# Counting a state space product as 6.0 units instead of 2.2 when attention tiles are handed out beside it

## The chip, the core and the metric

The kernel runs on one core of a Trainium2 chip, in one launch. The metric is the device time of that launch in microseconds (us); smaller is better. Engines are named as the profile names them: PE (TensorE, matmuls and transposes), DVE (VectorE), ACT (ScalarE), POOL (GpSimd) and SP (SyncE, which here only issues DMAs). L757 is line 757 of the kernel before.

## The reference, cut to what matters

Two layers of a small model on `x` of shape (2, 1024, 256), float32. Each of the four blocks reads a layer norm of `x` and is added to `x`:

```
x = x + attention(ln(x))      # 16 heads of 128, causal, linear bias by key position
x = x + ternary_ffn(ln(x))    # gated, hidden width 1024, weights quantized per group of 64
x = x + state_space(ln(x))    # in_proj 256->1024, conv of 4 taps, 512 channels x 16 states
x = x + kept_two_ffn(ln(x))   # gated, 1024 wide, of every 4 hidden values the 2 largest are kept
```

The state space block runs, for every channel d and state n, the recurrence

```
h[t] = exp(delta[t] * A[d, n]) * h[t-1] + delta[t] * B[t, n] * u[t, d]
y[t, d] = sum over n of h[t] * C[t, n]
```

Attention of a query needs all earlier keys of its sequence; the three other blocks need only the rows themselves and, for the state space, the state carried from the rows before.

## The kernel before

**Chunks and stages.** The 2 x 1024 rows are cut into four chunks of 512 rows: chunks 0 and 1 are the first and second half of sequence 0, chunks 2 and 3 those of sequence 1. Attention (`attention`, a generator) runs over the chunks in order, inside a chunk over 16 heads, inside a head over 4 tiles of 128 queries: 64 tiles to a chunk. One tile is scores on PE (L362), a clip with the mask on DVE (L366), the bias added and the row's extreme taken on DVE (L372, one instruction with two operands in SBUF), the exponential on ACT (L377), and two tiles later the transposes on PE (L293). Once a head there come the values (L304), the output projection (L318), its addition to `x` on DVE (L324), and the projections to q, k and v of the next head (L335, L342). Chunks 1 and 3 look back over 512 to 1024 keys and are called heavy here; chunks 0 and 2 look back over up to 512 keys and are called light.

While attention works on chunk k, the three other blocks of chunk k-1 (`rest`, also a generator) are interleaved with it. So there are five stretches: stage 0 (attention of chunk 0 beside the quantization of weights), stages 1, 2 and 3 (attention of chunks 1, 2 and 3 beside `rest` of chunks 0, 1 and 2), and a last stretch with `rest` of chunk 3 alone. In stage 1 and stage 3 the attention is heavy, in stage 2 it is light.

**What `rest` holds.** `ternary_ffn`: weights from DRAM through POOL's queue (L459), layer norm, 8 gated pieces (L441, `g_f` and `u_f`), and 64 matmuls back to width 256 (L502, `fo`). `state_space`: layer norm, `in_proj` (L608), the convolution as 4 DVE instructions for each of 4 channel groups (L624, L626), `dtl` and `bcp` (L639, L648), then `steps` for each channel group (a chain over PE, ACT, DVE and POOL, L544 to L575), then the 64 products (4 channel groups x 16 states), then the output projection (L816, `mo`). `kept_two_ffn`: layer norm, 8 gated pieces (L441, `g_g` and `u_g`), 6 comparisons (L924) and 12 further instructions on DVE (`keep_two`, L880 to L882), then the projection (L932, `go`) and the store of the result.

**A product** passes all engines: a row of B and a row of C are loaded, each spread over 128 partitions (SP's queue), `enter` multiplies on POOL (L736, `db`), `decay` makes the factors on ACT (L750, `da`), `scan` runs the recurrence on DVE (L757, `hs`), `keep` copies the last column on DVE (L766) where the sequence goes on, `weigh` multiplies by C on POOL (L771, `hc`), and `total` adds up on PE with 4 transposing matmuls (L701, `y`). These steps are staggered: `total` of a product is emitted 5 or 6 products after its `decay` (`DRAIN`).

**What sets the order.** Both generators say how far they are. The driver at L970 to L978 takes one tile of attention at a time, and after tile i of 64 runs `rest` until its emitted units reach the share (i + 1)/64 of the whole:

```
            whole = cost(k - 1)
            while done < whole * (i + 1) / (H * UT):
                done += next(r, whole)
```

Every `yield` in `rest` gives its units: 3 for a gated piece of the first ffn, 4 for one of the last, 2 for a quarter of an output projection, 2.2 for each product. `cost` (L952) adds up the same units for a whole `rest`. This order of emission is not yet the order on the engines: a scheduler builds each engine's instruction list from it, taking first what was emitted first among what it holds to be ready, and `tc.issue_after` adds constraints (a scan is held behind the L372 of the tile before the last one). Each engine then works through its own list in order. Weights of a block are loaded when the space of the block before is free.

Of the kernel before, what the change touches and what calls it, by code (L numbers as in the profile page):

```python
# [20 lines left out]
KC = D // P  # L21
NT = S // P
LAG = 2
FF = 1024
NFC = FF // P
GRP = 64
DI, DN, DR, DC = 512, 16, 128, 4
NDC = DI // P
NX = DR + 2 * DN
U = 512  # L30
UT = U // P
# [10 lines left out]
def kernel(  # L42
# [108 lines left out]

    guT_d = dr.tile([P, KC, 2 * FF], F32, tag="guT_d", name="guT_d")
    prT_d = dr.tile([P, NFC, D], F32, tag="prT_d", name="prT_d")

    def quantize(pool, key, src):
# [19 lines left out]
        yield  # L175
        q = pool.tile([P, n], BF16, tag="q", name=f"q_{key}", bufs=2 * FF // (2 * P) + FF // D)
        m = pool.tile([P, n], BF16, tag="m", name=f"m_{key}")
# [8 lines left out]
    def quantized_weights(pool):  # L186
        def put(key, q, dst):
# [12 lines left out]
            (f"gu{r}", w_gu[r : r + 2 * P, :].rearrange("(a p) d -> p a d", p=P), guT_d[:, :, r : r + 2 * P])  # L200
            for r in range(0, 2 * FF, 2 * P)
        ] + [
# [3 lines left out]
            )  # L206
            for c in range(0, FF, D)
        ]
# [77 lines left out]
    def turn(k, h, j, s, st):  # L286

        qi = CH[k][1] * UT + j
        for kb0 in range(0, qi + 1, 4):
            n = min(4, qi + 1 - kb0)  # L290
            tp = ps_mm(f"pt_{k}_{h}_{j}_{kb0}").rearrange("p (c t) -> p c t", c=4)
            for i in range(n):
                nc.tensor.transpose(  # L293
                    tp[:, i, :], s[:, (kb0 + i) * P : (kb0 + i + 1) * P], ident
                )
            nc.any.tensor_copy(st["pts"][kb0 // 4][:, 0:n, j * P : (j + 1) * P], tp[:, 0:n, :])  # L296

    def values(k, h, st):
        u = CH[k][1]
        zp = ps_z(f"z_{k}_{h}")  # L300
        last = (u + 1) * UT - 1
        for kb in range(last + 1):
            q0 = max(0, kb - u * UT) * P
            nc.tensor.matmul(  # L304
                zp[:, q0:], lhsT=st["v_all"][:, kb, :],
                rhs=st["pts"][kb // 4][:, kb % 4, q0:], start=(kb == 0), stop=(kb == last),
            )
        st["z"] = a2.tile([P, U], F32, tag="z", name=f"zs_{k}_{h}")
        nc.any.tensor_copy(st["z"], zp)  # L309

    def project(k, h, st):

        rr = a3.tile([P, UT], F32, tag="rr", name=f"rr_{k}_{h}")
        nc.vector.reciprocal(rr, st["rs"])
        for t in range(0, UT, 2):
            op = ps_mm(f"o_{k}_{h}_{t}").rearrange("p (a m) -> p a m", a=2)
            for i in range(2):
                ended["by"] = nc.tensor.matmul(  # L318
                    op[:, i, :], lhsT=st["z"][:, (t + i) * P : (t + i + 1) * P], rhs=st["o"],
                    start=True, stop=True,  # L320
                )
            for i in range(2):
                xt = x[k][:, t + i, :]
                nc.vector.scalar_tensor_tensor(  # L324
                    xt, op[:, i, :], rr[:, t + i : t + i + 1], xt, op0=ALU.mult, op1=ALU.add
                )
# [28 lines left out]
    def scores(k, h, j, st):  # L355

        W = (CH[k][1] * UT + j + 1) * P
        s = a3.tile([P, S], F32, tag="s", name=f"ss_{k}_{h}_{j}", bufs=4)
        for k0 in range(0, W, 512):
            n = min(512, W - k0)  # L360
            sp = ps_s(f"s_{k}_{h}_{j}_{k0}")
            nc.tensor.matmul(  # L362
                sp[:, :n], lhsT=st["qT"][:, j * P : (j + 1) * P], rhs=st["kT"][:, k0 : k0 + n],
                start=True, stop=True,
            )
            nc.vector.scalar_tensor_tensor(  # L366
                s[:, k0 : k0 + n], sp[:, :n], CLIP, lower[:, S - W + k0 : S - W + k0 + n],
                op0=ALU.min, op1=ALU.max,
            )
        nm = a3.tile([P, 1], F32, tag="nm", name=f"nm_{k}_{h}_{j}")  # L370
        pace["front"] = tiles[-2] if len(tiles) >= 2 else None
        pace["tile"] = nc.vector.tensor_tensor_reduce(  # L372
            out=s[:, :W], in0=s[:, :W], in1=st["alibi"][:, :W], scale=1.0,
            scalar=3.0e38, op0=ALU.add, op1=ALU.min, accum_out=nm,
        )
        tiles.append(pace["tile"])
        nc.scalar.activation(  # L377
            s[:, :W], s[:, :W], AF.Exp, bias=nm, scale=-1.0, accum_out=st["rs"][:, j : j + 1]
        )
        return s  # L380

    def attention():
# [7 lines left out]
        for i, (k, h) in enumerate(heads):  # L390
# [8 lines left out]
            for j in range(UT):  # L399
                s = scores(k, h, j, st)  # L400
                later.append((LAG, lambda a=(k, h, j, s, st): turn(*a)))
                if j == UT - 1:
                    later.append((LAG, lambda a=(k, h, st): values(*a)))
                    later.append((LAG + 1, lambda a=(k, h, st): project(*a)))
                if j == UT - 1 and h == H - 1:
# [45 lines left out]
    def ternary_ffn(k):  # L451
        with ExitStack() as fctx:
# [3 lines left out]
            f2 = fctx.enter_context(tc.tile_pool(name="f2", bufs=2, side="right"))  # L456
            guT = fw.tile([P, KC, 2 * FF], F32R, name=f"guT_{k}")
            prT = fw.tile([P, NFC, D], F32R, name=f"prT_{k}")
# [56 lines left out]
    DRAIN = lambda k: 5 if k + 1 < len(CH) and CH[k + 1][1] == 0 else 6  # L515

    def state_space(k):
# [5 lines left out]
        with ExitStack() as mctx:  # L523
# [20 lines left out]
            def steps(c):  # L544

                vp = ps_r(f"dt_{k}_{c}")
                ended["by"] = nc.tensor.matmul(
                    vp, lhsT=dt_sb[:, c * P : (c + 1) * P], rhs=dtl, start=True, stop=True
                )


                v = row_of("sv", f"sv_{k}_{c}", 1)
                e = row_of("se", f"se_{k}_{c}", 1)
                with tc.issue_after(marks[0].ins):
                    nc.scalar.activation(e, vp, AF.Abs, bias=dt_bias(c))
                relu = lambda: nc.scalar.activation(v, vp, AF.Relu, bias=dt_bias(c))

                idle = tail_end and c == 0
                if not idle:
                    relu()  # L560
                nc.scalar.activation(e, e, AF.Exp, scale=-1.0)
                l = row_of("dl", f"dl_{k}_{c}", 2)
                log = nc.scalar.activation(l, e, AF.Ln, bias=one)
                if idle:
                    with tc.issue_after(log.ins):
                        relu()
                r = work(f"sr_{k}_{c}")
                nc.vector.tensor_scalar(r, e, 1.0, -1.0, ALU.add, ALU.add)  # L568
                marks.append(nc.vector.tensor_tensor(r, e, r, ALU.subtract))
                (nc.vector if idle else nc.gpsimd).tensor_tensor(l, l, r, ALU.add)  # L570
                dl = l
                (nc.vector if short or idle else nc.gpsimd).tensor_tensor(dl, v, l, ALU.add)
                du = row_of("du", f"du_{k}_{c}", 2)
                marks.append((nc.vector if idle else nc.gpsimd).tensor_tensor(du, dl, xs[:, c, :], ALU.mult))
                return dl, du  # L575

            def turned(c, du):

                tp = ps_r(f"dup_{k}_{c}")
                for t in range(UT):  # L580
                    nc.tensor.transpose(
                        tp[:, t * P : (t + 1) * P], du[:, t * P : (t + 1) * P], ident
                    )
                duT = row_of("duT", f"duT_{k}_{c}", 2)
                nc.scalar.copy(duT, tp)
                return duT
# [213 lines left out]
            for i in range(-5, len(prods) + DRAIN(k)):  # L800
                for lag, f in stages:
                    if 0 <= i - lag < len(prods):
                        f(i - lag)
                if i >= 0:
                    yield 2.2
                if 0 <= i < len(prods) and i // DN + 1 < NDC:
                    c = i // DN + 1
                    if i % DN == (DN // 4 if tail_end else DN // 2):
                        parts[c] = steps(c)
                        yield 3  # L810
                    if tail_end and i % DN == DN - 5:
                        turns[c] = turned(c, parts[c][1])
# [134 lines left out]
    def rest(k):  # L947
        yield from ternary_ffn(k)
        yield from state_space(k)
        yield from kept_two_ffn(k)  # L950

    def cost(k):  # L952

        own = 3 + 3 * NFC + 2 * UT + 3 + 5 * NDC + 4 + 3 * NDC + 2.2 * (DN * NDC + DRAIN(k)) + 2 * UT
        return own + 3 + 4 * NFC + 1.3 * 6 + 2.5 * 4 + 4 * UT


# [90 lines left out]
```

## Time and profile before

| | us |
|---|---|
| median of 3 runs | 1836.12 |
| lowest and highest run | 1835.04, 1838.70 |
| span of the profiled execution, first to last instruction | 1836.9 |
| PE busy | 1718.3 (94% of the span) |
| DVE busy | 1218.3 (66%) |
| ACT busy | 963.7 (52%) |
| POOL busy | 832.2 (45%) |

The page gives no time of the profiled execution beside its span; the span lies between the lowest and the highest run, so nothing of note lies around it. A share of busy time is a mean over stretches with different limits, so the stretches have to be read one by one. Two cautions go with PE: its instructions are pipelined and overlap in the records, so the mean duration of a matmul is more than the distance from its start to the next one's, and gaps shorter than that overlap are counted as busy. In the answers below "mean ns" is the recorded duration of one instruction, and "x" the number of records; a float32 matmul makes two records.

### The profile page before, as it was taken

What the parts mean: (1) busy time and instruction counts of PE and PEld (TensorE: products, weight loads), DVE (VectorE), ACT (ScalarE), POOL (GpSimd) and SP (SyncE); (2) the same over time, 40 slices, a digit from 0 to 9 for tenths busy, and PEclk for the clock granted to TensorE, in tenths of its full rate; (3) what the DMA queues carried; (4) which work ended last, traced back from release to release, by engine and by line L of the source; (5) the groups of instructions that cost most, each with busy time, mean ns of one, the idle gap of its engine ahead of it and who ended that gap; (6) DMA issues with size and microseconds to landing.
All of it is one profiled execution on the core that took longest, in us unless ns stands there. A gap on an engine that the chain in (4) does not pass through costs nothing. (4 is left out here: it accounts for less than half of the span.)

```text
span 1836.9 us, 24217 instructions
## 1 busy us (share of the span) xinstructions
PE 1718.3 (94%) x7956; PEld 1144.2 (62%) x7956; DVE 1218.3 (66%) x2349; ACT 963.7 (52%) x1789; POOL 832.2 (45%) x674
## 2 busy tenths in 40 slices
PE   7999999998999999998888999999999999998899
PEld 4666666555656557755555667756656565566895
DVE  5666555777785473458886565557788655667975
ACT  3444474656563553555554545566555446446742
POOL 3324032588892000419998000418898500035870
PEclk9999999999999999999999999999999999999999
DMA  6443512466662311337787324227665430212541
GB/s 201 128 142 128 193 46 88 149 203 204 216 202 91 103 52 48 125 109 232 245 247 224 116 71 141 82 67 228 226 214 184 142 115 26 75 53 86 178 136 57
DMA packets 178301, 255.99 MB, mean 139 GB/s; under 512 B 16240, under 2 KB 90992, under 8 KB 177152
## 3 DMA queue, kind: packets, MB, share of 16 engines
q1 hardware_dynamic: 176752, 241.61, 41.4%
q0 software_dynamic: 1152, 12.58, 1.9%
q8 instruction: 63, 1.03, 0.2%
q14 instruction: 62, 0.51, 0.1%
q10 hardware_dynamic: 272, 0.26, 0.0%
HBM read 232.04 MB, written 22.35 MB: 138 GB/s over the span
## 5 line engine op out<-in xcount | busy, mean ns | idle before, releaser
L771 POOL TENSOR_TENSOR hc<-hs,cs 128x512 f32<-128x512 f32 x256 | 362.1, 1428 | 10.8 <-DVE ss L366 3.1
L362 PE MATMUL s<-kT,qT 128*128 128x512 f32 (+3 forms) x768 | 302.7, 495 | 19.9 <-DVE ss L366 18.0
L377 ACT ACTIVATE ss<-ss,nm 128x128 f32<-128x128 f32 (+7 forms) x256 | 198.8, 776 | 183.5 <-DVE nm L372 174.1
L366 DVE SCALAR_TENSOR_TENSOR ss<-s,lower 128x512 f32<-128x512 f32 (+3 forms) x384 | 204.6, 549 | 121.0 <-PE s L362 119.4
L736 POOL TENSOR_TENSOR db<-du,bs 128x512 f32<-128x512 f32 x192 | 259.2, 1356 | 44.4 <-DVE hs L757 30.6
L304 PE MATMUL z<-pT,v 128*128 128x512 f32 (+3 forms) x768 | 264.5, 492 | 10.9 <-ACT pT L296 10.2
L372 DVE CUSTOM_DVE_ANT_0 ss<-ss,alibi 128x128 f32<-128x128 f32 (+7 forms) x256 | 241.3, 945 | 3.5
L750 ACT ACTIVATE da<-dl,a_neg 128x512 f32<-128x512 f32 x256 | 177.9, 698 | 115.6 <-DVE hs L757 90.6
L304 PEld LDWEIGHTS z<-pT,v 128*128 128x128 f32 x768 | 142.8, 190 | 145.1 <-issue 92.7
L296 ACT COPY pT<-pt 128x512 f32<-128x512 f32 (+3 forms) x321 | 145.4, 474 | 162.0 <-PE pt L293 160.4
L293 PE MATMUL pt<-ident,ss 128*128 128x128 f32 x1152 | 180.3, 279 | 32.1 <-DVE x L324 18.5
L293 PEld LDWEIGHTS pt<-ident,ss 128*128 128x128 f32 x1152 | 140.0, 142 | 94.7 <-DVE x L324 33.0
L362 PEld LDWEIGHTS s<-kT,qT 128*128 128x128 f32 x768 | 127.9, 193 | 84.1 <-issue 43.4
L757 DVE TENSOR_TENSOR_SCAN hs<-da,db 128x512 f32<-128x512 f32 x128 | 153.8, 1210 | 38.6 <-ACT da L750 20.8
L757 DVE TENSOR_TENSOR_SCAN hs<-da,carry,db 128x512 f32<-128x512 f32 x128 | 159.1, 1269 | 24.4 <-POOL hc L771 14.7
L324 DVE SCALAR_TENSOR_TENSOR x<-o,rr,x 128x256 f32<-128x256 f32 x256 | 108.9, 476 | 76.7 <-PE o L318 76.5
L701 PE MATMUL y<-ident,hc 128*128 128x128 f32 x1024 | 144.8, 279 | 8.4 <-POOL hc L771 8.4
L342 PEld LDWEIGHTS pv<-wv,xT_a 128*128 128x128 f32 x1024 | 124.4, 192 | 37.1 <-issue 25.3
L342 PE MATMUL pv<-wv,xT_a 128*128 128x128 f32 x1024 | 125.8, 275 | 5.5 <-ACT zs L309 3.4
L701 PEld LDWEIGHTS y<-ident,hc 128*128 128x128 f32 x1024 | 121.0, 145 | 14.3 <-POOL hc L771 11.9
L318 PE MATMUL o<-wo,zs 128*128 128x256 f32 x512 | 125.4, 386 | 4.1 <-ACT kT L338 3.0
L335 PE MATMUL pq<-xT_a,wq 128*128 128x512 f32 x256 | 122.7, 601 | 0.7 <-ACT xT_a L148 0.7
(204 smaller groups left out, 2468.7 us busy)
## 6 DMA issues: line engine op xcount, KB each, us to landing
cs<-bcd SPq DMA_DIRECT2D x256, 256.0 KB, 3.8
bs<-bcd SPq DMA_DIRECT2D x192, 256.0 KB, 4.3
alibi<-alibi_d SPq DMA_DIRECT2D x32, 512.0 KB, 4.2
wq<-in_wqT_dram SPq DMA_DIRECT2D x64, 128.0 KB, 3.5
wk<-in_wkT_dram SPq DMA_DIRECT2D x64, 128.0 KB, 3.1
wv<-in_wvT_dram SPq DMA_DIRECT2D x64, 128.0 KB, 2.8
wo<-in_woT_dram SPq DMA_DIRECT2D x64, 128.0 KB, 2.8
alibi<-alibi_d SPq DMA_DIRECT2D x32, 256.0 KB, 3.6
```

Source lines behind the costliest of these rows:

```text
L293: nc.tensor.transpose(tp[:, i, :], s[:, (kb0 + i) * P : (kb0 + i + 1) * P], ident)
L304: nc.tensor.matmul(zp[:, q0:], lhsT=st["v_all"][:, kb, :], rhs=st["pts"][kb // 4][:, kb % 4, q0:], start=(kb == 0), stop=(kb == last),)
L342: nc.tensor.matmul(vp[:, t, :], lhsT=xT[:, c, t * P : (t + 1) * P], rhs=st["v"][:, c, :], start=(c == 0), stop=(c == KC - 1),)
L362: nc.tensor.matmul(sp[:, :n], lhsT=st["qT"][:, j * P : (j + 1) * P], rhs=st["kT"][:, k0 : k0 + n], start=True, stop=True,)
L366: nc.vector.scalar_tensor_tensor(s[:, k0 : k0 + n], sp[:, :n], CLIP, lower[:, S - W + k0 : S - W + k0 + n], op0=ALU.min, op1=ALU.max,)
L372: pace["tile"] = nc.vector.tensor_tensor_reduce(out=s[:, :W], in0=s[:, :W], in1=st["alibi"][:, :W], scale=1.0, scalar=3.0e38, op0=ALU.add, ...
L377: nc.scalar.activation(s[:, :W], s[:, :W], AF.Exp, bias=nm, scale=-1.0, accum_out=st["rs"][:, j : j + 1])
L701: nc.tensor.matmul(yTs[c][:, t * P : (t + 1) * P], lhsT=h[:, t * P : (t + 1) * P], rhs=ident, is_transpose=True, start=start and t == 0, s ...
L736: nc.gpsimd.tensor_tensor(db[i], du, brow.pop(i), ALU.mult)
L750: nc.scalar.activation(da[i], parts[c][0], AF.Exp, scale=a_neg[:, c, n : n + 1])
L757: nc.vector.tensor_tensor_scan(out=hs[i], data0=da.pop(i), data1=db.pop(i), initial=0.0 if first else carry[:, n, c : c + 1], op0=ALU.mult ...
L771: nc.gpsimd.tensor_tensor(hc[i], hs.pop(i), crow.pop(i), ALU.mult)
```

## The change

A named constant takes the place of the literal 2.2, in both places that have to agree: in what `state_space` yields after each product, and in what `cost` adds up for it. Its value is 6.0. No instruction is added, removed or altered by it; it decides after which attention tile each piece of `rest` is emitted. By the driver's arithmetic a whole `rest` goes from about 305 units to about 571, a tile's share from 4.8 to 8.9 units, and the products with the `steps` between them from about 35 of the 64 tiles of a stage to about 48. The two ffns, the first half of the state space block and its output projection keep their units and so get fewer tiles.

```
--- before.py
+++ after.py
@@ -21,6 +21,7 @@
 KC = D // P
 NT = S // P
 LAG = 2
+PRODUCT = 6.0
 FF = 1024
 NFC = FF // P
 GRP = 64
@@ -802,7 +803,7 @@
                     if 0 <= i - lag < len(prods):
                         f(i - lag)
                 if i >= 0:
-                    yield 2.2
+                    yield PRODUCT
                 if 0 <= i < len(prods) and i // DN + 1 < NDC:
                     c = i // DN + 1
                     if i % DN == (DN // 4 if tail_end else DN // 2):
@@ -951,7 +952,7 @@
 
     def cost(k):
 
-        own = 3 + 3 * NFC + 2 * UT + 3 + 5 * NDC + 4 + 3 * NDC + 2.2 * (DN * NDC + DRAIN(k)) + 2 * UT
+        own = 3 + 3 * NFC + 2 * UT + 3 + 5 * NDC + 4 + 3 * NDC + PRODUCT * (DN * NDC + DRAIN(k)) + 2 * UT
         return own + 3 + 4 * NFC + 1.3 * 6 + 2.5 * 4 + 4 * UT
```

More of the change, by code (lines that the diff above doesn't have):

```diff
@@ L23 @@
 LAG = 2
+PRODUCT = 6.0
 FF = 1024
@@ L804, in state_space @@
                 if i >= 0:
-                    yield 2.2
+                    yield PRODUCT
                 if 0 <= i < len(prods) and i // DN + 1 < NDC:
@@ L952, in cost @@
     def cost(k):
-        own = 3 + 3 * NFC + 2 * UT + 3 + 5 * NDC + 4 + 3 * NDC + 2.2 * (DN * NDC + DRAIN(k)) + 2 * UT
+        own = 3 + 3 * NFC + 2 * UT + 3 + 5 * NDC + 4 + 3 * NDC + PRODUCT * (DN * NDC + DRAIN(k)) + 2 * UT
         return own + 3 + 4 * NFC + 1.3 * 6 + 2.5 * 4 + 4 * UT
```

## The prediction

> **What bounds the kernel now.** I read the stages first, then in the stages the waits. Cut at the first and the last product total of each stage, every stage has a stretch A (first ffn, first half of the state space block), B (the products) and C (output projection, last ffn). The busy times by stretch, A B C of stages 1, 2, 3:
>
> ```profile
> core 0: us, PE busy (x) PEld busy (x) DVE busy (x) ACT busy (x) POOL busy (x), PEclk, DMA share, GB/s
> 230.00:364.00 134.00, 131.07 (x558) 81.80 (x557) 81.67 (x166) 85.14 (x136) 44.83 (x41) 1.00 0.28 89
> 364.00:588.00 224.00, 205.69 (x999) 135.86 (x998) 169.71 (x302) 124.11 (x226) 175.95 (x126) 1.00 0.60 189
> 588.00:732.00 144.00, 143.54 (x576) 89.48 (x575) 75.76 (x155) 69.69 (x111) 2.02 (x2) 1.00 0.21 69
> 732.00:833.00 101.00, 97.01 (x425) 63.39 (x424) 57.52 (x142) 56.96 (x113) 35.20 (x33) 0.99 0.37 121
> 833.00:1013.00 180.00, 147.87 (x746) 105.34 (x745) 143.35 (x211) 93.53 (x194) 166.24 (x128) 0.94 0.77 236
> 1013.00:1119.00 106.00, 104.27 (x433) 68.41 (x432) 56.18 (x135) 48.69 (x92) 2.26 (x2) 1.00 0.28 94
> 1119.00:1253.00 134.00, 132.14 (x549) 83.22 (x548) 80.20 (x165) 79.65 (x131) 45.68 (x43) 0.97 0.35 112
> 1253.00:1476.00 223.00, 205.37 (x996) 135.53 (x994) 168.74 (x302) 123.77 (x226) 176.28 (x126) 1.00 0.59 191
> 1476.00:1606.00 130.00, 125.44 (x485) 74.86 (x483) 71.90 (x140) 64.30 (x104) 3.03 (x3) 1.00 0.21 75
> ```
>
> In all A and C stretches PE is busy for 96 to 100% of the time: it is the bound there. Only in B does it idle, and most in stage 2, where POOL is busy for 166 of 180 us. Next the waits of PE inside B, two of stage 1 and two of stage 2:
>
> ```profile
> PE s L362 <- DVE ss L366: 8.5, 9, 1.3
> PE pt L293 <- DVE x L324: 4.9, 4, 1.6
> ```
> ```profile
> PE y L701 <- POOL hc L771: 7.9, 7, 3.0
> PE pt L293 <- DVE x L324: 7.8, 5, 2.4
> ```
>
> In the heavy stage PE waits for a DVE that is late with attention because scans stand in its queue; in the light one it also waits for POOL's product. Then the chain of waits, for the price of PE's work at full rate:
>
> ```profile
> 1582.66 5.59 PE z L304 x16
> 1589.76 1.73 PE o L318 x8
> 1645.50 13.97 PE in L608 x32
> ```
>
> So a float32 record of 512 columns costs 0.43 us (13.97 / 32), less for fewer columns; from one start to the next the timeline gives 0.216 for 256 columns, 0.109 for 128, 0.231 for a matmul of the first ffn's gated pieces, 0.120 for one of its `fo`. A heavy head: values 5.6, scores the same, transposes 26 x 0.109 = 2.8, output 1.7, q and k 3.4, v 16 x 0.111 = 1.8, in all 20.9, or 5.2 us a tile. A light head has 1280 instead of 3328 columns in scores and values and 10 transposes: 12.2, or 3.1 us a tile. A product's total is 4 x 0.109 = 0.44.
>
> **PE's need against the time.** Adding these prices over PE's list of before gives, for A, B, C: stage 1: 128.0, 198.7, 141.4; stage 2: 91.6, 131.1, 102.6; stage 3: 124.9, 198.7, 123.0. Against the windows PE idles 6, 25, 3; 9, 49, 3; 9, 24, 7: 136 us in 1376, and 98 of them in the three B.
>
> **What moves.** The order of the changed program, laid against that of before, shows how many tiles each stretch gets: A 16 becomes 11, 13, 11; B 32 becomes 44, 42, 44; C 16 becomes 9. (The first ffn keeps its tiles; its matmuls wait for weights that cannot be loaded before the last block has left.) Need after, added from the new list in the same way: stage 1: 105.3, 260.9, 103.4; stage 2: 81.2, 165.2, 80.7; stage 3: 100.3, 260.9, 83.7. The sum is 1241.6 against 1240.0. Nothing is saved in work; the change is worth what it does to 136 us of idle time.
>
> **B, heavy (stages 1 and 3).** Twelve tiles more, 62 us of PE, while the products stay 64. DVE in B of before: 64 scans, copies and steps are 85 of 170 us, 32 tiles the other 85, so 2.65 a tile and 1.33 a product. Per head of 4 tiles DVE had 10.6 + 8 x 1.33 = 21.2 us against 24.8 of PE (198.7 / 8), and has 10.6 + 5.8 x 1.33 = 18.3 against 23.7 (260.9 / 11). Counted by heads from the starts in the timeline, the idle time of PE is uneven: 1.5 us in heads with 9 scans and no `steps`, 4.6 in those where `steps` puts 1.8 us more into DVE's queue (L568, L569). With three such heads at about 3 us and eight at 0.4 I take 12 us, so 273. Bounds: 5 (nothing left but the steps) to 34 (each head goes on idling for 3.1).
>
> **What speaks against it: POOL and DVE collide.** The bias instruction L372 beside POOL (B of stage 1) and without it (C of stage 1), then POOL's own two in B:
>
> ```profile
> L372 DVE CUSTOM_DVE_ANT_0 ss<-ss,alibi 128x1024 f32<-128x1024 f32 x8 | 14.1, 1757 | 0.0
> ```
> ```profile
> L372 DVE CUSTOM_DVE_ANT_0 ss<-ss,alibi 128x1024 f32<-128x1024 f32 x5 | 6.1, 1218 | 0.0
> ```
> ```profile
> L771 POOL TENSOR_TENSOR hc<-hs,cs 128x512 f32<-128x512 f32 x61 | 92.4, 1519 | 3.0 <-DVE ss L366 1.5 <-PE y L701 1.3
> L736 POOL TENSOR_TENSOR db<-du,bs 128x512 f32<-128x512 f32 x56 | 77.2, 1382 | 18.3 <-DVE hs L757 13.6 <-DMA bs<-bcd 4.8
> ```
>
> A tile moved into B costs DVE up to 0.54 us more (the 2.65 hold it already), and lengthens POOL's instructions, which take 1.26 at best: over 64 products (0.26 + 0.12) x 64 = 24 us for 32 tiles, 0.76 a tile. Twelve tiles: up to 6 us of DVE and 9 of POOL. In a heavy B of 273 us all have room (DVE 44 x 2.65 + 85 = 202, POOL 176 + 9 = 185, ACT, 124 of 224 before, less), so I add nothing. [...]
>
> **B, light (stage 2).** POOL sets the pace: 64 x (1.36 + 1.34) plus three times 2.6 for the steps is 180.6, the measured 180. Ten tiles more bring PE to 165, DVE from 143 to 143 + 10 x 1.42 = 157 (45.4 us of attention over 32 tiles), POOL by 10 x 0.36 (its excess over 1.26, 11.5 us, over 32 tiles) to 184. Three engines above 80% that each work through a list in order will not reach 184. I take 194, nearer to the pace of POOL than to the sum: bounds 180 (all fits) and 208 (DVE's 14 us and POOL's 4 come end to end, and POOL's waits for rows, 5 us before at a DMA share of 0.77, triple). Idle time of PE 29 instead of 49.
>
> The granted clock is 0.94 in this B and 1.00 or nearly so in most others. [...]
>
> **A and C: cover taken away.** Here the removed tiles hid waits.
> - After `fo`, x is updated, normalized, transposed. Before, 3.3 us of attention stood there and the step from `fo` to `in_proj` took 8.2 us; after, 1.3 us stand there. The last stretch, without attention, does it in 5.3. New idle 1 to 3, twice (stage 2 keeps its tiles).
> - `in_proj` runs with almost no tile: 15 us of PE beside 4 x (0.48 + 3 x 0.75) = 10.9 of convolution on DVE. The last stretch takes 13.8 from `in_proj` to `dtl`, so 1 to 2 us new.
> - In stage 2 the first product total stands 18 us of PE after the start of `dtl`, and it took 24 before: 6 us idle instead of 4.
> - Before the last ffn's gated pieces again a layer norm: 1.5 to 2 new.
> - After the gated pieces DVE has 3 x 1.22 of comparisons and 4 x (0.69 + 0.69 + 1.22) of `keep_two`, 14 us. The new list has 19, 13 and 25 us of PE before `go`: covered, but for 2 to 4.
>
> With the old idle of the first ffn that is A 9, 15, 13 and C 7, 8, 11: 63 instead of 37 (bounds 45 and 85). SP issues the loads of 11 heads instead of 8 between the rows of B and C; heavy B falls in rate with its length, and in light B it is in the 208.
>
> **The sum.** Stage 1: 114 + 273 + 110 = 497 against 502. Stage 2: 96 + 194 + 89 = 379 against 387. Stage 3: 113 + 273 + 95 = 481 against 487. Together 19 us less; stage 0 and the last stretch keep their order. From the span 1836.9 that is 1818; the span agrees with the median 1836.1 within what a measurement of this kernel can tell, about 0.2% or 3.7 us, so nothing is added.
>
> **Rivals.**
> - Slower: idle time goes with the tiles. If every heavy head goes on idling for 3.1 us (scans bunched in front of L366, `ps_s` with two banks), both heavy B keep 34 us, B together 97 instead of 98, and the 26 us lost in A and C plus 1.6 of need stay: 1862. It decides from 21 us of idle in each heavy B, 2 us a head. For it: DVE's list of after still bunches up to four scans. Against: heads without `steps` idle for 1.5 us at 9 scans already.
> - Faster by more: heavy B idle 5 each, light B 18 (183 us), A and C at their lower bound 45: 28 + 45 against 136, and 1.6: 1775. For it: PE reaches 98 to 100% wherever DVE has room. Against: the last stretch's own gaps.
> - No difference: it does less than it says. 44 tiles lie in B and not 48, and the first ffn is not thinned; if A and C lose what B wins (heavy B 17, light B 35), the time stays within 3.7 us.
>
> **How the numbers follow.** The forecast's own range, with the middle of each bound, is 1800 to 1832. Chances: forecast 0.50, faster by more 0.16, no difference 0.10, slower 0.24. So faster 0.66, same 0.10, slower 0.24. The range 1791 to 1850 leaves out about half of each outer rival.
>
> **What would show it.** Right: B of stages 1 and 3 about 273 us with PE's need at 95%, B of stage 2 about 194 with the clock nearer to 1, A and C of all stages shorter by 12 to 35 us except A of stage 2, L372 in B at 1.6 to 1.8 us for 1024. Wrong: waits of `s` on L366 in the heavy B over 15 us, POOL's `hc` above 1.6 us in stage 2, or gaps of several us ahead of `in`, `g_g` and `go`.

## The result and the profile after

The changed kernel takes 1847.09 us (median of four runs, 1844.88 to 1848.93) against 1835.92 (1835.04 to 1838.70) for the kernel before beside it. The ratio is 1.0062, with a 95% interval of 1.0047 to 1.0076: 0.6% slower, where 1818 us was forecast. The profiled execution of after has a span of 1847.1 us, against 1836.9.

The busy times by stretch again, A B C of stages 1, 2, 3, for the kernel after:

```profile
core 0: us, PE busy (x) PEld busy (x) DVE busy (x) ACT busy (x) POOL busy (x), PEclk, DMA share, GB/s
230.00:345.00 115.00, 109.29 (x457) 68.85 (x456) 72.31 (x148) 72.04 (x113) 46.21 (x43) 0.99 0.31 95
345.00:631.00 286.00, 268.46 (x1271) 176.52 (x1270) 202.60 (x368) 149.56 (x278) 169.55 (x124) 1.00 0.52 163
631.00:738.00 107.00, 105.34 (x411) 65.63 (x409) 61.65 (x127) 41.62 (x67) 2.58 (x3) 1.00 0.19 64
738.00:833.00 95.00, 86.37 (x372) 56.48 (x372) 48.55 (x111) 55.93 (x103) 33.80 (x33) 0.98 0.37 120
833.00:1041.00 208.00, 181.53 (x906) 126.62 (x906) 166.73 (x265) 109.32 (x235) 167.67 (x128) 0.95 0.69 220
1041.00:1125.00 84.00, 82.40 (x327) 53.32 (x325) 49.07 (x117) 29.37 (x58) 3.03 (x3) 1.00 0.29 93
1125.00:1234.00 109.00, 105.59 (x441) 66.21 (x440) 67.94 (x132) 66.55 (x109) 46.47 (x45) 0.98 0.38 128
1234.00:1520.00 286.00, 270.55 (x1266) 179.03 (x1265) 201.40 (x367) 148.94 (x276) 168.50 (x123) 0.99 0.50 159
1520.00:1617.00 97.00, 89.58 (x316) 51.69 (x315) 54.10 (x101) 39.60 (x63) 2.90 (x3) 0.96 0.21 77
```

The tiles moved as planned, so B grew and A and C shrank everywhere. What matters is by how much. The three B (heavy, light, heavy) came to 286, 208 and 286 us where 273, 194 and 273 were forecast; POOL's share of the light B fell from 166 of 180 to 168 of 208, so POOL no longer sets its pace.

To split each stretch into need and idle time I priced every matmul at its distance from start to start at full rate (the prices of the prediction) and called idle what a distance exceeds that by, if it is over 60 ns. Each idle piece is put down to the matmul that ends it. Where the granted clock is below 1.00, matmuls start further apart (those of 128 columns 0.213 us from 852.7 to 862.9 us of after, where the clock stood at 0.50, against 0.110 at 1.00), and that counts as idle too: by an estimate from the clock of the rows, up to 11 us in the light B before (0.94 of 180 us), up to 10 after (0.95 of 208), and up to 3 in the heavy B of stage 3 after (0.99 of 286). In us, with the forecast in brackets:

| | need before | need after | idle before | idle after |
|---|---|---|---|---|
| B of stage 1 | 198.7 | 261.0 | 24.0 | 23.4 (12) |
| B of stage 2 | 131.1 | 165.3 | 47.5 | 41.8 (29) |
| B of stage 3 | 198.7 | 261.0 | 23.4 | 24.1 (12) |
| the three A | 346.1 | 288.2 | 27.4 | 35.1 (37) |
| the three C | 369.2 | 268.4 | 10.7 | 18.1 (26) |
| together | 1243.8 | 1243.9 | 133.0 | 142.5 (116) |

Need is unchanged to 0.1 us. Idle time rose by 9.5 us, and the nine stretches together by 10.0, which is the whole loss: stage 0 (228.6 and 228.8 us) and the last stretch (230.7 and 230.6) stayed. The loss lies in A and C, which idle 15.1 us more; the light B gives 5.7 back, and the two heavy B, which were to give 25 by the forecast, give nothing.

Which instruction ended the idle time is the line that I had not drawn up for before. In heavy B of before, scores `s` ended 12.1 of the 24.0 us, transposes `pt` 6.0, values `z` 3.6; a product's total `y` ended 0.7. After, scores ended 17.1 of 23.4 and values 5.3. Almost all of it is attention waiting for attention's own steps on DVE and ACT. That tells which instruction came late, not yet what made it late. In light B of before, `pt` ended 17.6, `y` 13.2, `z` 6.3 and `o` 4.5 of 47.5; after, 13.0, 8.5, 10.5 and 5.2 of 41.8.

The waits of B of stage 1 (engine, line and what it waited for: us in total, times, longest), two of DVE's before:

```profile
DVE ss L366 <- PE s L362: 22.2, 13, 12.2
DVE v L347 <- PE pv L342: 15.9, 2, 8.0
```

and after:

```profile
DVE ss L367 <- PE s L363: 80.6, 19, 11.7
POOL hc L772 <- PE y L702: 39.3, 6, 11.8
PE s L363 <- DVE ss L367: 13.2, 11, 2.2
PE z L305 <- ACT pT L297: 3.1, 4, 1.0
```

PE and DVE wait for each other by turns: DVE stands 81 us ahead of the masks (22 before, and 16 ahead of copies of v), PE 13 us for them (8.5 before). The recorded wait of 13.2 is less than the 17.1 from start to start because short gaps vanish in the overlap of matmul records (one of scores over 512 columns lasts 0.61 us on the mean there, and at full rate the next starts 0.43 us after its start). The same for the light B:

```profile
PE y L702 <- POOL hc L772: 5.2, 5, 2.2
PE z L305 <- ACT pT L297: 4.2, 4, 1.9
PE pt L294 <- DVE x L325: 3.2, 2, 2.9
```

How the turns come about is seen in the timeline of one heavy head, first PE, then DVE (start, duration, what, count, and in brackets the idle time before it and its releaser):

```profile
434.14 1.12 PE L363 MATMUL s<-kT,qT 128*128 128x512 f32 x2 [0.76 <-DVE ss L367]
435.10 5.82 PE L305 MATMUL z<-pT,v 128*128 128x512 f32 x16
440.76 1.88 PE L336 MATMUL pq<-xT_a,wq 128*128 128x512 f32 x4
442.48 1.88 PE L336 MATMUL pk<-xT_a,wk 128*128 128x512 f32 x4
444.52 2.05 PE L343 MATMUL pv<-wv,xT_a 128*128 128x128 f32 x16 [0.16 <-ACT zs L310]
446.41 0.81 PE L363 MATMUL s<-kT,qT 128*128 128x384 f32 x2
...
461.12 1.12 PE L363 MATMUL s<-kT,qT 128*128 128x512 f32 x2 [1.34 <-DVE ss L367]
```
```profile
443.14 0.27 DVE L767 COPY carry<-hs 128x1 f32<-128x1 f32 x2
447.26 0.56 DVE L367 SCALAR_TENSOR_TENSOR ss<-s,lower 128x384 f32<-128x384 f32 x1 [3.84 <-PE s L363]
...
450.60 2.32 DVE L758 TENSOR_TENSOR_SCAN hs<-da,db 128x512 f32<-128x512 f32 x2
452.84 1.26 DVE L367 SCALAR_TENSOR_TENSOR ss<-s,lower 128x512 f32<-128x512 f32 x2
454.14 2.10 DVE L373 CUSTOM_DVE_ANT_0 ss<-ss,alibi 128x1024 f32<-128x1024 f32 x1
```

From 435.1 to 446.4 PE works off the values of one head and q, k and v of the next, 11.3 us in which DVE gets no new scores and runs dry (3.84 us here; its eleven stands of 3.4 to 11.7 us in this stretch, one a head, all lie at that place). The same run stands in each head of before; there more scans and products per head were at hand (64 products to 32 tiles and not to 44). Then scores come again, and DVE has masks, the bias (2.10 us beside POOL, against 1.22 in stretch C of before) and held-back scans at once; with two banks for scores PE stands before the next one, at 461.1 for 1.34 us.

### The profile page after: what moved, and what is told of

It is laid out like the page before. It is cut to its first block, busy times and chain, and to the rows that moved or that the text cites. A ratio compares the mean times of both kernels' runs of the same rounds, so it can differ in the third digit from the quotient of the medians.

```text
span 1847.1 us, 24242 instructions
## 1 busy us (share of the span) xinstructions
PE 1724.5 (93%) x7956; PEld 1150.4 (62%) x7956; DVE 1236.4 (67%) x2365; ACT 930.1 (50%) x1757; POOL 821.2 (44%) x674
## 5 line engine op out<-in xcount | busy, mean ns | idle before, releaser
L772 POOL TENSOR_TENSOR hc<-hs,cs 128x512 f32<-128x512 f32 x256 | 347.6, 1370 | 111.4 <-PE y L702 94.4
L363 PE MATMUL s<-kT,qT 128*128 128x512 f32 (+3 forms) x768 | 303.6, 498 | 28.3 <-DVE ss L367 27.4
L373 DVE CUSTOM_DVE_ANT_0 ss<-ss,alibi 128x128 f32<-128x128 f32 (+7 forms) x256 | 252.5, 988 | 3.4
L297 ACT COPY pT<-pt 128x512 f32<-128x512 f32 (+3 forms) x310 | 139.0, 470 | 128.3 <-PE pt L294 127.2
L702 PE MATMUL y<-ident,hc 128*128 128x128 f32 x1024 | 151.4, 279 | 5.5 <-POOL hc L772 5.4
```

What stands on the lines that cost most here:

```text
L363: nc.tensor.matmul(sp[:, :n], lhsT=st["qT"][:, j * P : (j + 1) * P], rhs=st["kT"][:, k0 : k0 + n], start=True, stop=True,)
L373: pace["tile"] = nc.vector.tensor_tensor_reduce(out=s[:, :W], in0=s[:, :W], in1=st["alibi"][:, :W], scale=1.0, scalar=3.0e38, op0=ALU.add, ...
L702: nc.tensor.matmul(yTs[c][:, t * P : (t + 1) * P], lhsT=h[:, t * P : (t + 1) * P], rhs=ident, is_transpose=True, start=start and t == 0, s ...
L772: nc.gpsimd.tensor_tensor(hc[i], hs.pop(i), crow.pop(i), ALU.mult)
```

## The experiments

"Need" and "idle" are counted as above; each ratio is to the kernel before, run beside it, with its 95% interval. Edits are to the kernel after unless another is named.

**One kind of stage alone.** First the heavy stages at 6.0 and the light one at 2.2, then the reverse (`PRODUCT(k)` where it is used).

```diff
-PRODUCT = 6.0
+PRODUCT = lambda k: 6.0 if k % 2 == 0 else 2.2    # heavy alone; light alone: k % 2 == 1
```

> 6.0 units a product where the attention beside it is heavy (stages 1 and 3), 2.2 in stage 2. Read stage by stage from the two traces, stage 1 grew by 6.4 us and stage 3 by 4.3, stage 2 by none. If the stages are independent the time is 1847 us, 11 over the kernel before. If the loss sits in the light stage, or in what one stage leaves to the next, it is 1838 or less.

> 6.0 units a product in stage 2 alone, 2.2 in stages 1 and 3. If the stages are independent: 1836 us, no difference from before (stretch B of stage 2 longer by 28 us, A and C shorter by 29). If the light stage carries a loss that its borders hide: 1840 or more.

Heavy alone: 1852.37 us, 1.0082 (1.0069 to 1.0095); idle 23.4 and 24.6 in its heavy B, 47.8 in its light one. Light alone: 1839.27 us, 1.0008 (0.9999 to 1.0016); idle 43.0 in the light B, 23.3 and 24.0 in the others. So the whole loss is in the heavy stages, and there in A and C, since their B idle as before; what the light B wins is spent in its A (idle 16.4 instead of 9.3) and by need that moved across the borders. The heavy stages alone lose more than all three together (1.0082 against 1.0062, with intervals that just overlap), so the stages are probably not independent.

**Is it the scans in front of the masks?** `paced` ties each scan to be issued after a named instruction of attention. Without it the scheduler places the scans freely.

```diff
-            paced = not tail_end
+            paced = False
```

> The changed kernel without the constraint that holds a scan behind the L372 of the tile before the last one. The built list of DVE then has 46 of the 64 scans of a heavy stage in the stretch where PE works on values and projections, instead of 34, and 18 instead of 30 in front of the masks of the other tiles. Theory (PE idles in the heavy B because DVE's list has scans in front of the masks that PE waits for, while DVE stood idle just before): idle time of PE in each heavy B falls from 24 us to 12 or less, waits of the scores on the masks from 17 us to 8, time 1820 to 1828. Rival (POOL's collision with L372 makes DVE late, whatever the order) and rival (idle time goes with the number of tiles): both B stay within 3 us, time 1845 to 1849.

1911.80 us, 1.0403 (1.0389 to 1.0418). The heavy B idle 43.0 and 40.9 us instead of 23.4 and 24.1; scores ended 19.0, output `o` 7.6, `v` 6.7. The tie was worth over 60 us here, and the theory that it is what makes the masks late was wrong. (At granted clocks of 0.97 over 305 us and 0.96 over 303, up to 9 and 12 us of the idle time in these two B are slower matmuls, by the same estimate.)

**A share by weight.** The rest of the work is handed out in unequal portions after the four tiles of a head, 0.2, 2.8, 0.6 and 0.4 shares, so that most of it follows the second tile, where the long run stands.

```diff
+HANDED = (0.2, 3.0, 3.6, 4.0)
-            while done < whole * (i + 1) / (H * UT):
+            while done < whole * (i // UT * UT + HANDED[i % UT]) / (H * UT):
```

> The changed kernel with the units handed out unevenly over the four tiles of a head: 0.2, 2.8, 0.6 and 0.4 tile shares instead of 1 each, so that most products are emitted with the second tile, where PE has values and projections. DVE's list has 42 of 64 scans there instead of 34, and 4 instead of 12 after the third tile. Theory of the order: idle time of PE in each heavy B from 24 to 14 or less, time 1824 to 1832. Rivals collision and number of tiles: heavy B unchanged within 3 us, 1845 to 1849. In the light stage POOL works evenly and a bunched emission may cost: up to 8 us there under every theory.

1845.60 us, 1.0041 (1.0026 to 1.0056); the heavy B idle 19.3 and 30.3, the light one 48.0. One heavy B won 4.1 us, the other lost 6.2. Its 30.3 us hold one wait of 8.1 us at its start, behind a bias over 896 columns that took 10.00 us on DVE (1.20 on the mean in B of stage 1 after) while POOL ran its products without a gap. No gain.

**Splitting the long run.** q, k and v of the next head are emitted after the last tile instead of after the second, which parts them from the values. Tried at 6.0 for all heads, at 2.2 for all heads (on the kernel before), and at 6.0 for heavy heads alone.

```diff
-                if j == 1 and i + 1 < len(heads):
+                if j == 3 and i + 1 < len(heads):              # all heads
+                if j == (3 if u else 1) and i + 1 < len(heads):  # heavy heads alone
```

> The changed kernel with the projections to q, k and v of the next head emitted after the fourth tile of a head instead of the second. In a heavy head PE's 13 us in a row of values and projections, in which it asks nothing of DVE, become two of 6 and 5 us. Theory (with two banks of scores PE cannot work ahead for DVE, so in each head DVE stands idle for the long run of projections and is then late for the short tiles; the idle time belongs to the head): idle time of PE in each heavy B from 24 us to 12 or less, DVE's idle time ahead of the masks from 81 us to 50 or less, time 1820 to 1828. Rivals (POOL's collision with L372, or PE waiting on the products themselves): heavy B within 3 us of before, 1844 to 1850.

> The kernel before with the same move of the projections to after the fourth tile. Theory of the head: idle time in each heavy B from 24 us to 16 or less (the heads with steps keep theirs), time 1818 to 1828. Rivals: 1833 to 1840.

> The changed kernel with the projections of the next head after the fourth tile where attention is heavy, after the second where it is light. In the run that moved all of them stage 1 took 498 us and stage 3 481 instead of 509 and 491, while stage 0 lost 13 us and stage 2 8. If the stages are independent: 1847 - 11 - 10 = 1826 us, 0.5% under the kernel before. If the gain of the heavy stages was borrowed from the stages between: 1837 or more.

At 6.0, all heads: 1848.89 us, 1.0060 (1.0047 to 1.0073). The heavy B fell to 13.3 us of idle each, from 23.4 and 24.1, but stage 0 lost 13 us (241.8 before stage 1 instead of 228.8), and the light B went to 47.9. At 2.2 the same move made things worse, against what I expected: 1877.20, 1.0217 (1.0197 to 1.0238), heavy B idle 35.3 and 30.3, of which values ended 20.7 and 16.3. At 6.0 for heavy heads alone it is **1830.79 us, 0.9964 (0.9951 to 0.9976)**: faster than both kernels. Its three B:

```profile
345.00:617.00 272.00, 261.04 (x1245) 172.45 (x1244) 199.41 (x357) 148.44 (x274) 172.01 (x124) 1.00 0.53 169
824.00:1032.00 208.00, 182.33 (x902) 127.48 (x903) 167.18 (x264) 109.55 (x234) 168.30 (x129) 0.94 0.70 221
1227.00:1497.00 270.00, 260.99 (x1242) 172.12 (x1241) 197.05 (x356) 148.03 (x275) 164.16 (x120) 1.00 0.52 165
```

and two waits of its B of stage 1:

```profile
DVE ss L367 <- PE s L363: 61.8, 30, 6.9
PE z L305 <- ACT pT L297: 6.6, 6, 1.7
```

The longest stand of DVE fell from 11.7 to 6.9 us, and scores end only 0.4 us of PE's idle time instead of 17.1; values now end 9.1. Idle is 15.1 and 13.3 us in the heavy B, 125 in all against 142.5, while the light B keeps 41.6.

**Is it DVE's load?** A product by 1.0 on `o` in PSUM ahead of the update of x, in heavy heads, lengthens DVE's list and changes no value.

```diff
+                if CH[k][1]:
+                    nc.vector.tensor_scalar(op[:, i, :], op[:, i, :], 1.0, None, ALU.mult)
```

> The changed kernel with four more DVE instructions a heavy head (each output tile of attention is first multiplied by 1.0 in PSUM, about 0.4 us each, 1.6 us a head), in the place where the chain of masks begins. If PE's idle time in the heavy B is lateness of DVE with attention: each heavy B grows by 12 to 18 us (11 heads), the time by 25 to 50. If PE waits there on something else: under 6 us a stretch, under 15 in all.

One run: 1849.14 us. In B of stage 1 the added instructions took 16 us, and the bias was faster than after's 1787 ns:

```profile
L326 DVE TENSOR_SCALAR o<-o 128x256 f32<-128x256 f32 x42 | 16.3, 426 | 12.7 <-PE o L319 12.7
L375 DVE CUSTOM_DVE_ANT_0 ss<-ss,alibi 128x1024 f32<-128x1024 f32 x11 | 14.4, 1313 | 0.1
```

The heavy B idle 20.4 and 18.4, less than after. But DVE's load hardly rose: it is busy for 204.7 us in this B against 202.6, because the bias was faster and copies of transposes (L297) went to ACT, and the lists were built anew (DVE's idle time ahead of the masks is 55 instead of 81 us). So this run doesn't test a heavier DVE; the next four say more.

**Is it the collision of DVE and POOL?** Two edits take it away from the bias (at 6.0 its 1024 columns in B of stage 1 then take 1.23 and 1.21 us instead of 1.79), each at 6.0 and at 2.2 (the second on the kernel before): the product with C on POOL left out, together with the loads of its rows of C, and with more buffers for the scan's results, which are then read in its place; and the bias left out, its minimum taken by a DVE instruction with one SBUF input. For comparison the bias and the product in B of stage 1 of the kernel after:

```profile
L373 DVE CUSTOM_DVE_ANT_0 ss<-ss,alibi 128x1024 f32<-128x1024 f32 x11 | 19.7, 1787 | 0.0
L772 POOL TENSOR_TENSOR hc<-hs,cs 128x512 f32<-128x512 f32 x60 | 84.9, 1415 | 47.0 <-PE y L702 39.3 <-DVE hs L758 5.1 <-DMA cs<-bcd 2.5
```

```diff
-                nc.gpsimd.tensor_tensor(hc[i], hs.pop(i), crow.pop(i), ALU.mult)
+                hc[i] = hs.pop(i)
```
```diff
-        pace["tile"] = nc.vector.tensor_tensor_reduce(
-            out=s[:, :W], in0=s[:, :W], in1=st["alibi"][:, :W], scale=1.0,
-            scalar=3.0e38, op0=ALU.add, op1=ALU.min, accum_out=nm,
+        pace["tile"] = nc.vector.tensor_scalar(
+            s[:, :W], s[:, :W], 0.0, None, ALU.add, ALU.min, accum_out=nm,
```

> The changed kernel without the multiplication by C on POOL (left out, with its rows of C: the totals add up h itself). POOL's work in B halves. If the collision with POOL makes DVE late: L372 of 1024 columns falls from 1.7 towards 1.4 us and the idle time of PE in each heavy B from 24 us to 14 or less. Theory of the head: heavy B keeps 19 us or more. In the light B, where PE waits on products and POOL on PE, idle time falls from 42 us to 25 or less if POOL's share is what couples them, and stays over 35 if the lists' order is.

> The kernel before without the multiplication by C on POOL, as in the run that left it out of the changed kernel (1783.9 us beside 1839 of the kernel before). If the collision is what ate the gain: 1790 to 1805, slower than the changed kernel without it. If it takes as much from both: 1770 to 1778, and the changed one stays 8 us or more behind.

> The changed kernel with the bias by key position left out: the instruction that added it and took the row's extreme on DVE (two operands in SBUF) becomes one that reads its single operand from SBUF and takes the extreme. POOL's work, rows and chains stay. Theory (in the heavy B the collision of L372 with POOL falls on PE: without POOL's weighing the idle time went from 24 to 11 us and DVE's work fell by 15): the instruction takes the same time with and without POOL beside it, POOL's two fall towards 1.27 us, idle time of PE in each heavy B from 24 to 10 to 15 us, time 1805 to 1822. Rival (what mattered when the weighing was left out was POOL's load, the rows and the chain, not the collision): heavy B keeps 20 us or more, time 1838 or more.

> The same in the kernel before. If the collision is what ate the gain of the change, it eats less here (fewer tiles beside POOL): idle time in each heavy B from 24 to 14 to 18 us, time 1815 to 1825, so that 6.0 units are then equal to or faster than 2.2. If not, 6.0 stays 8 us or more behind 2.2 without the bias as well.

Without the product: 1783.90 us (one run) at 6.0, 1780.18 at 2.2 (0.9681, 0.9666 to 0.9696). At 6.0 the heavy B idle 11.0 and 10.9, the light one 17.3; at 2.2 13.5, 13.5 and 15.1. In B of stage 1 at 6.0, the bias:

```profile
L373 DVE CUSTOM_DVE_ANT_0 ss<-ss,alibi 128x1024 f32<-128x1024 f32 x11 | 13.6, 1234 | 0.0
```

DVE still stood 83 us ahead of the masks there, and yet PE idled only 11. So DVE running dry is not by itself what costs PE. But 2.2 gains about as much as 6.0 from the product's absence, and even with POOL half empty 6.0 is no faster than 2.2.

Without the bias: 1850.34 us at 6.0 (1.0080, 1.0051 to 1.0108), 1843.17 at 2.2 (1.0030, 1.0020 to 1.0040): no gain, though the bias no longer collided. In B of stage 1 at 6.0, DVE and then POOL:

```profile
L373 DVE TENSOR_SCALAR_CACHE_REDUCE ss<-ss 128x1024 f32<-128x1024 f32 x11 | 13.3, 1207 | 0.0
```
```profile
L771 POOL TENSOR_TENSOR hc<-hs,cs 128x512 f32<-128x512 f32 x61 | 77.8, 1275 | 70.3 <-PE y L701 61.7 <-DVE hs L757 4.1 <-DVE x L325 2.9
```

Scores ended 9.8 instead of 17.1 us of idle, about what the product's absence made of it (7.9); but values rose to 8.1 and transposes to 5.6, and B idled 25.8 and 31.5 us in all (the profiled execution, span 1861.2, is the slowest of its four). At 2.2 the heavy B idle 23.2 and 23.1. So scores wait less without the bias's collision, but its absence alone brings nothing. The two edits at 2.2 also say something of DVE's load: in B of stage 1 DVE is busy for 157.3 us without the bias and 157.8 without the product, against 169.7 before; PE's need is the same in all three, and its idle time 23.2, 13.5 and 24.0 us. The same load of DVE goes with both.

**Other weights.** 3.5 and 10.0 for the product's units; then 3.5 with the split run, and the split run with 2.2 in the light stage.

```diff
-PRODUCT = 6.0
+PRODUCT = 3.5      # or 10.0; the last run: lambda k: 6.0 if k % 2 == 0 else 2.2
```

> 3.5 units a product: about 37 tiles between the first and the last product total of a heavy stage, between the 32 of before and the 44 of the changed kernel. Theory (PE's gaps in B end with attention's own instructions, so more attention does not fill them): idle time in each heavy B 20 to 28 us as at both ends, A and C in between, time 1838 to 1844. Rival (it is the order that the scheduler happened to build): idle time in the heavy B outside 18 to 30.

> 10 units a product: about 48 tiles in the heavy B, 44 or more in the light one. Theory: idle time in each heavy B 20 to 28 us and in the light one 38 to 48, nothing filled; A and C lose 3 to 10 us more cover, time 1848 to 1860. If more attention does fill: heavy B 15 or less, time 1840 or less.

> 3.5 units, and the projections of the next head after the fourth tile where attention is heavy. With 6.0 units that took heavy B's idle time from 24 to 14 us, with 2.2 it raised it to 33, because the values then waited for their transposed tiles. In between: idle time of 15 to 30, time 1825 to 1850; under 1830 it beats the one with 6.0.

> Late projections in heavy heads with 6.0 units in stages 1 and 3 and 2.2 in stage 2. From the stages measured alone stage 2 costs the same with both values: 1828 to 1836 us, no difference from the one with 6.0 everywhere. If the borders of the light stage matter: outside.

| units | us | ratio | need of a heavy B | idle of heavy B | of light B |
|---|---|---|---|---|---|
| 2.2 (before) | 1835.92 | 1 | 198.7 | 24.0, 23.4 | 47.5 |
| 3.5 | 1862.93 | 1.0136 (1.0110 to 1.0162) | 226.8 | 26.3, 23.4 | 58.0 |
| 6.0 (after) | 1847.09 | 1.0062 (1.0047 to 1.0076) | 261.0 | 23.4, 24.1 | 41.8 |
| 10.0 | 1882.07 | 1.0233 (1.0206 to 1.0259) | 284.3 | 33.8, 36.3 | 43.3 |
| 3.5, split run | 1848.45 | 1.0054 (1.0037 to 1.0072) | 238.4 | 18.8, 15.9 | 52.1 |
| 6.0, split run | 1830.79 | 0.9964 (0.9951 to 0.9976) | 255.8 | 15.1, 13.3 | 41.6 |
| 6.0, light 2.2, split run | 1837.50 | 1.0004 (0.9991 to 1.0017) | 255.8 | 15.2, 13.5 | 47.8 |

From 2.2 to 6.0 a heavy B gets 62 us more of attention and its idle time does not move. At 10.0 it rises by about 11 us, and one wait in each heavy B is all of that: a bias took 10.76 us in stage 1 and 9.39 in stage 3 while POOL ran eight and seven of its products without a gap, and PE stood for 11.2 and 13.0 us until DVE had got past it. Of stage 1:

```profile
345.32 10.76 DVE L373 CUSTOM_DVE_ANT_0 ss<-ss,alibi 128x896 f32<-128x896 f32 x1
356.93 1.54 PE L294 MATMUL pt<-ident,ss 128*128 128x128 f32 x6 [11.15 <-DVE x L325]
```

Without these two waits 22.6 and 23.3 us are left, as at 2.2 and 6.0. The curve of the times is not smooth; each value has the scheduler build other lists, which probably is why, but no run shows it. In the last row A of stage 3, where the stages of different weight meet, idles 17.6 instead of 10.4, which with the fuller idle of the light B takes back the gain of the split run.

## Why the prediction was wrong

- **The step that failed** is "B, heavy": "three such heads at about 3 us and eight at 0.4 I take 12 us". It took DVE's load per head (21.2 us falling to 18.3) for the cause of the idle time, and supposed that a lighter DVE would be on time. No row gave the 0.4. Measured: 23.4 and 24.1 us, 2.15 a head. Counted from the first matmul of q of one head to that of the next, in B of stage 1, the three heads with `steps` idled for 1.3 to 1.8 us and the eight others for 2.3 on the mean, 0.3 to 3.6; one with 3 scans idled for 3.2 and one with 5 for 0.7, so PE did not wait less in a head with fewer scans. Idle time in B ended with attention's own instructions already before (23 of 24 us), and 62 us more of attention filled none of it. DVE's load alone doesn't set the idle time: at 2.2 some 157 us of DVE go with 23.2 us of it (no bias) and with 13.5 (no product). By the counts after, DVE has room on the mean (202 of 286 us) and is late in spells: dry for several us during values, q, k and v, then behind for several tiles. Splitting that run took 8 to 11 us of idle time from each heavy B while DVE's load hardly changed (197 to 199 us against 201 to 203), which speaks for the spells; that the same edit hurts at 2.2 keeps it from being a rule, and the spells stay an argument.
- **"B, light"** was too low too: 41.8 us of idle and not 29, a duration of 208 at the upper bound given. The reason named there fits: POOL fell from 166 of 180 to 168 of 208, and three engines at 80 to 87% that take turns did not reach POOL's pace. Still 5.7 us were won here.
- **"A and C"** held, and were a little too dark: 53 us of idle against 63 forecast and 38 before. The single steps in it I did not part. C of stage 1 and 2 lost next to nothing (2.9 and 2.5), while in C of stage 3 12.7 us stand, 6.1 of them ended by transposes.
- **The sum** by its terms: against the forecast 116 us of idle, the heavy B are 23.5 over, the light B 12.8, A and C 9.8 under, together 26.5; the span is 29 us over the forecast. What A and C came out under hid about a quarter of the miss in B, and as their steps were not measured one by one, that is luck.
- **The rivals.** The slower one named the side and the point: it "decides from 21 us of idle in each heavy B, 2 us a head", and 23.4 and 24.1 lie above. Its size did not hold, since each head idled for 2.15 and not 3.1 us and A and C lost 15 and not 26: 1847 instead of 1862. Its cause, scans bunched in front of the masks with two score banks, is half right. PE does wait for masks (13.2 us in 11 waits in B of stage 1 by the record), but scans freed of their tie made it worse (1912 us). Nothing of the faster one was seen.
- **The signs named in advance**: the bias with 1024 columns was to take 1.6 to 1.8 us and took 1.79; POOL's `hc` in stage 2 stayed under 1.6 (1.34); the waits of `s` on the masks were 13.2 and 12.8 us in the two heavy B by the record, short of the 15 that were to show the forecast wrong, which was set too high (from start to start scores ended 17.1 us of idle in stage 1). The heavy B at 286 instead of 273 us showed it.
- **The clock.** The light B was to come "with the clock nearer to 1". That was the author's estimate: the rows of before give 0.94 with 47.5 us of idle and 1.00 with 24.0 and 23.4, and no run shows what sets the clock. It went from 0.94 to 0.95, with 41.8 us of idle still spread over the stretch. With POOL's product left out at 6.0 and 17.3 us of idle, the same stretch has 0.99:

```profile
814.00:1000.00 186.00, 175.65 (x916) 124.21 (x917) 147.17 (x271) 111.65 (x240) 90.23 (x69) 0.99 0.54 164
```

There the clock was higher with fewer us of idle. The total of idle time alone does not set it: at 10.0 units the light B had 0.97 with 43.3 us. And by the record no wait of PE in the light B after was longer than 3.0 us, while the clock was 0.95.

**What stays open.** Why the product on POOL costs each heavy B 10 to 13 us is not parted into collision, POOL's load, the loads of the rows of C, the longer chain and the buffers: leaving the bias out removes its own collision alone and gains nothing. Why the split run helps at 6.0 and 3.5 and hurts at 2.2 is seen only as values that wait for transposed probabilities (20.7 us); the order that leads there was not isolated, because every edit rebuilds the lists.

## What to carry to other kernels

Before work is moved to fill idle time, list which instruction ends that idle time: here 23 of 24 us ended with the filler's own chain, and 62 us more of it filled nothing. The list does not name the cause, since the product on POOL, of the other chain, was worth 10 to 13 us of the same idle time. Then make the sum once with the idle time of the target stretch unchanged. The prediction's slower rival is that sum (1862 us, at 0.24); the forecast of a gain needed two drops that nothing had measured, 25 us in the heavy B and 20 in the light one, of which 0 and 5.7 came. A weight in a list scheduler is no smooth knob (1836, 1863, 1847 and 1882 us at 2.2, 3.5, 6.0 and 10.0), so a value between two measured ones says little.

## What the runs showed of the hardware

- DVE and POOL slowed each other, a little on the mean and much in single cases. The bias over 1024 columns, with two SBUF inputs, took 1.23 us with POOL's product left out (while POOL's other product ran on at 1.38) and 1.79 beside both, up to 2.29. With one SBUF input a like instruction took 1.21 beside POOL, and POOL's 512 columns 1.275 instead of 1.415. The mean loss here was 0.56 us, and the largest in the kernel after 1.07. Where POOL ran eight of its products without a gap, at 10.0 units, the bias over 896 columns took 10.76 us (1.20 on the mean in B of stage 1 after) and ended 1 us after the last of them.
- One SBUF input or two did not tell which DVE instruction took longer. The scan of the heavy stages, which has two, took 1.21 us in B of stage 1 after, both beside POOL (37 scans) and without it (9). The addition in `steps` (`sr<-se`), which has one, took 0.42 us in B of stage 1 with POOL's product left out and 1.64 with the bias left out and POOL at work on both its products, each the mean of three; at 2.2 units without the bias one took 7.28. First without the product, then without the bias:

```profile
L569 DVE TENSOR_SCALAR sr<-se 128x512 f32<-128x512 f32 x3 | 1.3, 424 | 1.6 <-ACT se L562 1.6
```
```profile
L568 DVE TENSOR_SCALAR sr<-se 128x512 f32<-128x512 f32 x3 | 4.9, 1641 | 0.9 <-ACT se L561 0.9
```

- The granted clock was lower in the heavy B too where idle time was larger: 0.97 and 0.96 with 43.0 and 40.9 us of idle (without pacing; by estimate up to 9 and 12 of them the slower clock's own), against 1.00 and 0.99 with 23.4 and 24.1.
